# Splitting sets of exponentials between ScalarE and VectorE in a graph-transformer kernel

## The chip, the cores and the metric

The kernel runs on one core of one Trainium2 chip. The metric is device time in microseconds (us): the median of several runs. Engines are named as in the profile: PE is TensorE's matmul, PEld its weight load, ACT is ScalarE, DVE is VectorE, POOL is GpSimd, SP is SyncE, whose queue issues most of the transfers (DMA).

## The reference

Four layers on one graph with N = 3327 nodes, 128 features and a dense float32 matrix `adj`. Each layer ends with a residual and a layer norm. Layer 0 is attention with 128 independent "depths" d and a contraction over 8 heads h; the adjacency is added to the scores twice:

```
h = Wq.shape[0] // d                      # 8
q = (x @ Wq.T).reshape(d, n, h)           # k, v alike
a = jnp.einsum('dnh,dmh->dnm', q, k) * scale
a = a + spatial_encoding + edge_encoding  # both are adj
a = jax.nn.softmax(a, axis=2)
out = jnp.einsum('dnm,dmh->dnh', a, v)
```

So 128 x 3327 x 3327 exponentials are needed, some 1.4 billion. Layers 1 to 3 are products of `adj` (or its transpose) with a 3327 x 128 matrix. Layer 1 scales by the roots of the row sums, layer 2 divides by row sums (`A @ X`) and by column sums (`A.T @ X`), layer 3 has no scaling.

## The kernel before

First a projection stage writes q, k (split into a high and a low part), v and the softmax's row maxima to DRAM. Then comes the attention stage, which this change is about, then a tail: the attention's division and output projection, and four sweeps over `adj`, each in 26 tiles of 128 rows.

**Attention.** A block is a range of CW = 476 queries and one of four ranges of keys (KBS: 7, 7, 6 and 6 tiles of 128 keys); seven query ranges make 28 blocks. Within a block the 128 depths are steps; four steps are a group (GROUP), three groups share one accumulation bank (PACK). In the texts a block with kb = 0 is called full, the other with seven tiles seven, and those with six tiles six. For each step the score tiles, keys on partitions and queries along the row, are made in three sets of PSUM banks `sc[0..2]` (SETS: 3, 2, 2 tiles, or 2, 2, 2). `exponents` does one set: score matmuls (line 632; keys of even and odd tiles stand on different halves of the rows, so two tiles run side by side), then one ACT instruction that takes exp of the whole set (line 640) into the SBUF tile `e`. At a block's first step transposes (line 625) put the adjacency into the banks, and later steps add to what stands there, with the query of the step before taken off again (rows 32 to 63 of `qt`, made by `copy_queries`, lines 517 to 519, in the full blocks and read back from DRAM in the others).

`weigh` does a round: one key tile, four depths, the exponentials times v into the bank `o` (line 658; each of the four column groups is recorded as two matmuls, so a round is x8). A queue holds the previous group's rounds; tables (FULL, PLACES, FIRST) say after which of a group's twelve sets how many rounds are issued. After three groups `flush` adds `o` to `acc` on DVE (lines 669 and 671). `store` writes the sums to `o_s` from POOL's queue.

**DVE's share of the exps.** In three of four groups of a full block, in all of a seven block and in seven of eight of a six block the group's first step gives its whole third set to DVE: `vector_exp` (line 596) reads the two score tiles from PSUM into `ey` as integers scaled for the exponent field, then two bit operations (597, 599) and five polynomial steps (602) follow, each on 128 x 952 elements. The follow-up steps wait in a list and are issued by `vector_work` when two simple clocks allow it.

**Background work.** In the same stage DVE transposes `adj` in 91 pieces of 512 x 256 (lines 218 to 233: transpose, maxima, row sums, column sums), which POOL's queue writes to `adjT_s` (line 253), one piece in eight groups.

**What sets the order.** In attention the order on PE, ACT, DVE and POOL is that of the program text; each instruction waits by semaphore for what it needs, and behind it its engine waits too. `load_heads` brings kt and qt two groups ahead on SP's queue. In the tail only PE and SP are ordered by hand. `gather` (line 1110) is one tile of a sweep: a load of 128 rows of `adjT_s` into one of five buffers, and 26 matmuls. In the first gather sweep DVE and ACT follow each tile with the residual and the norm (lines 1191 to 1077). Column sums are turned into shape before the tail by a small matmul (lines 1035 to 1043).

Of the kernel before, what the change touches and what calls it, by code (L numbers as in the profile page):

```python
# [12 lines left out]
I32 = mybir.dt.int32  # L13
# [17 lines left out]
POLY = (-0.12145248055458069, 1.287218689918518, 0.8447736501693726, 0.7106341123580933, 0.24892811477184296)  # L31
# [19 lines left out]
def kernel(ctx: ExitStack, tc: tile.TileContext, x, adj, wq, wk, wv, wo,  # L51
# [83 lines left out]
    colsum = const.tile([P, T], F32, name="colsum")  # L135
# [20 lines left out]
    csum = const.tile([P, NP // 32], F32, name="csum")  # L156
# [56 lines left out]
    def piece_work(pool, u, c, ai):  # L213

        nj = PIECE // 32
        w = min(PIECE, N - c * PIECE)
        at = pool.tile([P, nj, 4, 32], F32, name="at")
        nc.vector.transpose(at.rearrange("p j t b -> p t j b"), ai.rearrange("p t (j a) -> p t j a", a=32))
        yield at
        if c == 0:  # L220
            maxima[u] = pool.tile([P, 4, NPC], F32, name="pmax")
            sums[u] = pool.tile([P, 4, NPC], F32, name="psum")
        nc.vector.tensor_reduce(maxima[u][:, :, c], ai[:, :, 0:w], AX.X, ALU.max)
        yield at
        nc.vector.tensor_reduce(sums[u][:, :, c], ai[:, :, 0:w], AX.X, ALU.add)
        yield at
        part = csum[:, c * nj:(c + 1) * nj]
        if u == 1:
            nc.vector.tensor_reduce(part, at.rearrange("p j t b -> p j (t b)"), AX.X, ALU.add)
        else:  # L230
            cs = pool.tile([P, nj], F32, name="cs")
            nc.vector.tensor_reduce(cs, at.rearrange("p j t b -> p j (t b)"), AX.X, ALU.add)
            nc.vector.tensor_tensor(part, part, cs, ALU.add)
        yield at

    def store_tops(pool, u, top, n):

        hi = pool.tile([P, 4], F32R, name="rhi")
        nc.vector.tensor_copy(hi, top)
        lo = pool.tile([P, 4], F32R, name="rlo")  # L240
        nc.vector.tensor_tensor(lo, top, hi.bitcast(F32), ALU.subtract)
# [176 lines left out]
    def attention():  # L418
        with tc.tile_pool(name="ed", bufs=1) as ed, tc.tile_pool(name="kq", bufs=3) as kq, \
# [34 lines left out]
            def on_vector(kb, g):  # L454

                return g % 4 != 0 if kb == 0 else KBS[kb][1] == 7 or g % 8 != 0

            FULL = ((0, 2, 4, 4, 7, 7, 9), (0, 0, 3, 7, 7, 10, 10), (0, 0, 3, 6, 6, 9, 9), (0, 0, 3, 6, 7, 10, 10))
            PLACES = {7: (1, 1, 4, 6, 8, 10, 10), 6: (0, 2, 4, 6, 8, 10)}
# [50 lines left out]
            def copy_queries(b, g):  # L513
                qt = heads[b, g][1]
                qf = qt.bitcast(F32)
                before = heads[b, g - 1][1].bitcast(F32)[0:32, GROUP - 1] if g else qf[32:64, 0]
                return [(0.9, None, lambda: nc.vector.tensor_scalar(qt[32:64, 1:], qf[0:32, 0:GROUP - 1], -1.0, None, ALU.mult)),  # L517
                        (0.4, None, lambda: nc.vector.tensor_scalar(qt[32:64, 0], before, -1.0, None, ALU.mult)),
                        (1.2, None, lambda: nc.vector.tensor_copy(qt[64:128], qf[0:64]))]  # L519
# [22 lines left out]
            loaded, worked, turning = [], [], []  # L542

            def background(n):
                if n % PACE == 2 and worked:
                    piece_store(pe, *worked.pop(0))
                if n % PACE == 2 and pieces:
                    u, c = pieces.pop(0)
                    loaded.append((u, c, piece_load(pe, u, c)))

            def background_work(n):
                if n % PACE == 4 and loaded:
                    u, c, ai = loaded.pop(0)
                    steps = piece_work(pe, u, c, ai)
                    worked.append((u, c, next(steps)))
                    next(steps)
                    clock[1] += 2.4
                    turning.append(steps)
                if n % PACE == 0 and turning:
                    clock[1] += 2.4  # L560
                    for _ in turning.pop():
                        pass

            def prepare(b, d):

                n = b * NHG + d // GROUP
                if d % GROUP == 0:
                    while any(of is None for _, of, _ in vec):
                        vec.pop(0)[2]()
# [9 lines left out]
                    background(n)  # L579


                if n + 1 < len(groups) and blocks[groups[n + 1][0]][1] == 0 \
                        and d % GROUP == 1 - on_vector(blocks[b][1], d // GROUP):
                    vec.extend(copy_queries(*groups[n + 1]))
                if d % GROUP == 3:
                    background_work(n)

            vec = []

            def vector_exp(e, x, of):  # L590


                y = ex.tile([P, 2, CW], F32, name="ey")
                t = ex.tile([P, 2, CW], F32, name="et")
                yi, ti = y.bitcast(I32), t.bitcast(I32)
                nc.vector.tensor_scalar(yi, x, -58 * math.log(2.0), 2 ** 24 / math.log(2.0), ALU.max, ALU.mult)  # L596
                vec.append((0.7, of, lambda: nc.vector.tensor_scalar(ti, yi, UPPER, EXPONENT, ALU.bitwise_and,  # L597
                                                                 ALU.bitwise_xor)))
                vec.append((0.7, of, lambda: nc.vector.tensor_scalar(yi, yi, LOWER, QUARTER, ALU.bitwise_and,  # L599
                                                                 ALU.bitwise_or)))  # L600
                for i, a in enumerate(POLY):
                    vec.append((1.2, of, lambda i=i, a=a: nc.vector.scalar_tensor_tensor(  # L602
                        e, e if i else y, a, t if i == len(POLY) - 1 else y, ALU.add, ALU.mult)))

            clock = [0.0, 0.0]

            def vector_work(b):

                while vec and clock[1] < clock[0]:
                    cost, _, step = vec.pop(0)  # L610
                    step()
                    clock[1] += cost
                clock[0] += 0.95 if KBS[blocks[b][1]][1] == 7 else 0.84
                clock[1] = max(clock[1], clock[0] - 1)

            def exponents(b, d, si):
# [3 lines left out]
                s = sc[si]  # L620
                if d == 0:
# [14 lines left out]
                if on_vector(kb, d // GROUP) and (d % GROUP, si) == (0, 2):  # L636
                    vector_exp(e[:, 0:n, :], s[:, 0:n, 0:CW], (b, d // GROUP))
                    clock[1] += 1.2
                else:
                    nc.scalar.activation(e[:, 0:n, :], s[:, 0:n, 0:CW], AF.Exp, scale=2.0)  # L640
# [6 lines left out]
            def weigh(b, g, r):  # L647
# [5 lines left out]

                while any(of == (b, g) for _, of, _ in vec) and r >= SETS[len(queue_of)][2][0]:
                    vec.pop(0)[2]()
                for j in range(GROUP):
# [3 lines left out]
                                     start=(r == 0 and u == 0), stop=(r == nt - 1),  # L660
                                     skip_group_check=True)
                if r == nt - 1 and (u == PACK - 1 or g == NHG - 1):
                    flush(b, g // PACK)

            def flush(b, f):
                kb = blocks[b][1]
                clock[1] += 0.7
# [7 lines left out]
            def store(b, f):  # L675
                nb = min(PACK, NHG - f * PACK)
                for j in range(GROUP):
                    nc.gpsimd.dma_start(  # L678
# [6 lines left out]
            with tc.manual_schedule(engines={mybir.EngineType.PE, mybir.EngineType.Activation,  # L685
# [5 lines left out]
                for _, _, step in copy_queries(*groups[0]):  # L691
                    step()
                values[groups[0]] = load_values(*groups[0])
                for b, d in steps:
# [3 lines left out]
                    for si in range(len(SETS[KBS[blocks[b][1]][1]])):  # L698
                        vector_work(b)
                        exponents(b, d, si)  # L700
                        if queue:
                            at = (FIRST[len(queue_of)] if d < GROUP else PLACES[len(queue_of)] if blocks[b][1] else
                                  FULL[d // GROUP % 4])
                            for _ in range(at.count(place)):
                                weigh(*queue.pop(0))
                        place += 1
                    if d % GROUP == GROUP - 1:
                        while queue:
                            weigh(*queue.pop(0))
                        queue_of = [(b, d // GROUP, r) for r in range(KBS[blocks[b][1]][1])]  # L710
                        queue, place = list(queue_of), 0
                while queue:
                    weigh(*queue.pop(0))
                while stores:
# [320 lines left out]
    pick = act.tile([P, 32], F32, name="pick")  # L1035
    nc.vector.tensor_tensor(pick, ident[:, 0:32], ident[:, 32:64], ALU.add)
    nc.vector.tensor_tensor(pick, pick, ident[:, 64:96], ALU.add)
    nc.vector.tensor_tensor(pick, pick, ident[:, 96:128], ALU.add)
    ps = bank(7)
    nc.tensor.matmul(ps[0:32, 0:NP // 32], lhsT=pick, rhs=csum, start=True, stop=True)  # L1040
    for q in range(4):
        nc.vector.tensor_copy(colsum[32 * q:32 * q + 32, :],
                              ps[0:32, 0:NP // 32].rearrange("a (s q) -> a q s", q=4)[:, q, :])

# [17 lines left out]
    inv_col = inverse_degree(colsum, "inv_col")  # L1062
# [34 lines left out]

    def gather(t, y, col, b, meanwhile=()):
# [13 lines left out]
        for _, what in todo:  # L1112
            what()
        return ps
# [4 lines left out]
    def divide(t):  # L1119
# [7 lines left out]
        nc.gpsimd.tensor_tensor(ons[t][:n], o[:n, 0:H, :], rec[:n, :].unsqueeze(1).to_broadcast([n, H, D]), ALU.mult)  # L1127
# [38 lines left out]
    with tc.manual_schedule(engines={mybir.EngineType.PE, mybir.EngineType.SP}):  # L1166
# [18 lines left out]
        for t in range(T):  # L1185
# [9 lines left out]
            norm(n, h[:n, :], xs[1][:n, t, :])  # L1195

# [77 lines left out]
```

## Time and profile before

| what | us |
|---|---|
| runs, median of 3 | 10735.67 (10734.02 to 10740.07) |
| the profiled execution's own time | 10739.45 |
| its span in the profile | 10737.5 |
| ACT busy in the span | 9584.8 (89%) |
| PE busy | 10565.1 (98%) |
| DVE busy | 7960.2 (74%) |
| POOL busy | 1554.7 (14%) |
| first attention block starts | 316 |
| last flush of attention ends | 9970 |
| first, second, third gather sweep start | 10080, 10396, 10579 |

The granted clock of TensorE was 0.996 of full over the span. How to read the rows: a group of instructions has its line, engine and operation, the tile written and read, shapes and count; then busy time, the mean of one in ns; then the idle time of the engine just before them, and whose work ended it. In rows in order of time there are the start, the length, and the idle time before in brackets. Neighbouring instructions of one line are merged (x8, x16), so the length of a merged row runs from the first start to the last end. The recorded end of a matmul is modelled; its start is not.

### The profile page before, as it was taken

To read this page: it belongs to the slowest core of one execution; us is meant where nothing else is said; L and a number is where in the kernel's file an instruction comes from. 1 tells how busy PE (TensorE), PEld (TensorE's weight loads), DVE (VectorE), ACT (ScalarE), POOL (GpSimd) and SP (SyncE) were. 2 spreads that over 40 slices of the span, in tenths; PEclk is the share of its full clock that TensorE was granted. 3 is DMA by queue.
4 is the path that set the end of the run, shared out by engine and by line. 5 is a ranking of instruction groups with operands and counts; after the bars stand their busy time and mean duration, and the time that the engine had idled before them with its cause. 6 is when DMAs were issued, how large, how long until landed. Compare 5 with 4: busy or idle time off the path is not lost. (4 is left out here: it accounts for less than half of the span.)

```text
span 10737.5 us, 200822 instructions
## 1 busy us (share of the span) xinstructions
PE 10565.1 (98%) x76941; PEld 4105.8 (38%) x76941; DVE 7960.2 (74%) x8554; ACT 9584.8 (89%) x10447; POOL 1554.7 (14%) x2739
## 2 busy tenths in 40 slices
PE   8899999999999999999999999999999999999999
PEld 5333333333333333333333333333333333333779
DVE  6777888777888777887788777888777777777412
ACT  3899999999999999999999999999999999999400
POOL 0111121111221111211122110121111100001200
PEclk9999999999999999999999999999999999999999
DMA  7678886788876888768887588886888867788676
GB/s 270 181 184 188 209 210 181 181 192 201 213 188 171 198 201 209 190 166 200 198 211 196 156 191 191 199 199 172 193 195 202 193 162 179 181 189 196 219 283 246
DMA packets 1013760, 2116.43 MB, mean 197 GB/s; under 512 B 206759, under 2 KB 730985, under 8 KB 998979
## 3 DMA queue, kind: packets, MB, share of 16 engines
q1 hardware_dynamic: 932014, 1985.55, 74.4%
q0 software_dynamic: 79392, 116.16, 3.5%
q8 instruction: 623, 10.21, 0.4%
q14 instruction: 335, 2.74, 0.1%
q10 hardware_dynamic: 1396, 1.77, 0.1%
HBM read 1863.03 MB, written 239.54 MB: 196 GB/s over the span
## 5 line engine op out<-in xcount | busy, mean ns | idle before, releaser
L640 ACT ACTIVATE e<-sc 128x952 f32<-128x952 f32 (+1 forms) x9968 | 9360.0, 1085 | 312.1 <-PE sc L632 284.3
L658 PE MATMUL o<-e,v_pad 128*32 128x476 f32 (+1 forms) x46592 | 5647.1, 573 | 39.4 <-DVE acc L671 18.5
L632 PE MATMUL sc<-qt,kt 64*128 64x476 f32 x23296 | 4491.6, 440 | 52.9 <-ACT e L640 33.5
L632 PEld LDWEIGHTS sc<-qt,kt 64*128 64x128 f32 x23296 | 2184.3, 184 | 4433.6 <-ACT e L640 3740.6
L602 DVE SCALAR_TENSOR_TENSOR e<-e,ey 128x952 f32<-128x952 f32 x2352 | 2707.0, 1151 | 77.4
L596 DVE TENSOR_SCALAR ey<-sc 128x952 int32<-128x952 f32 x784 | 901.1, 1149 | 1411.5 <-PE sc L632 1389.9
L658 PEld LDWEIGHTS o<-e,v_pad 128*32 128x32 f32 (+1 forms) x46592 | 1035.2, 108 | 1907.4 <-issue 1885.1
L533 POOL COPY v_pad<-vs 128x192 f32<-128x192 f32 (+1 forms) x896 | 444.5, 522 | 8018.6 <-DMA vs<-v_img 6214.0
L602 DVE SCALAR_TENSOR_TENSOR e<-ey 128x952 f32<-128x952 f32 x784 | 903.4, 1152 | 27.2
L602 DVE SCALAR_TENSOR_TENSOR e<-e,et 128x952 f32<-128x952 f32 x784 | 901.2, 1149 | 22.3
L253 POOL DMA_DIRECT2D adjT_s<-at x1352 | 760.1, 570 | 132.7 <-DMA adjT_s<-at 92.6
L599 DVE TENSOR_SCALAR ey<-ey 128x952 int32<-128x952 int32 x784 | 519.7, 663 | 27.1
L597 DVE TENSOR_SCALAR et<-ey 128x952 int32<-128x952 int32 x784 | 518.3, 661 | 26.9
L1110 PE MATMUL bank<-y,eT 128*128 128x128 f32 (+1 forms) x4056 | 473.9, 276 | 0.4 <-DVE h L1232 0.4
L1110 PEld LDWEIGHTS bank<-y,eT 128*128 128x128 f32 (+1 forms) x4056 | 465.3, 192 | 5.7 <-DVE h L1232 0.6
L671 DVE TENSOR_TENSOR acc<-o,acc 128x476 f32<-128x476 f32 x231 | 150.3, 651 | 281.5 <-PE o L658 280.9
L517 DVE TENSOR_SCALAR qt<-qt 32x1428 fp32r<-32x1428 f32 x224 | 201.7, 900 | 103.2 <-DMA qt<-q_s 89.2
L519 DVE CAST qt<-qt 64x1904 fp32r<-64x1904 f32 x224 | 260.4, 1163 | 7.6
L1070 ACT ACTIVATE rstd<-mv,eps 128x1 f32<-128x1 f32 x104 | 30.4, 292 | 263.6 <-DVE mv L1068 263.6
L678 POOL DMA_DIRECT2D o_s<-acc x308 | 199.4, 651 | 35.4 <-DVE acc L671 20.8
L1213 PE MATMUL bank<-a,y 128*128 128x512 f32 (+2 forms) x364 | 145.5, 562 | 0.0
L362 ACT ACTIVATE hi<-pp 128x1024 fp32r<-128x1024 f32 x52 | 53.0, 1024 | 87.9 <-PE pp L308 86.3
(148 smaller groups left out, 2274.7 us busy)
## 6 DMA issues: line engine op xcount, KB each, us to landing
qt<-qimg SPq DMA_DIRECT2D x1344, 476.0 KB
kt<-k_s SPq DMA_DIRECT2D x5316, 96.0 KB
kt<-k_s SPq DMA_DIRECT2D x1762, 128.0 KB
eT<-adjT_s SPq DMA_DIRECT2D x78, 1664.0 KB
qimg<-qt SPq DMA_DIRECT2D x224, 476.0 KB
vs<-v_img SPq DMA_DIRECT2D x224, 224.0 KB
adjT_s<-at POOLq DMA_DIRECT2D x1352, 32.0 KB, 4.8
vs<-v_img SPq DMA_DIRECT2D x224, 192.0 KB
```

What stands on the lines that cost most here:

```text
L253: nc.gpsimd.dma_start(out=flat_ap(adjT_s, (t * P + 32 * q) * NP + c * PIECE, [[NP, 32], [P, ns], [1, P]]), in_=at[32 * i:32 * i + 32].rear ...
L517: return [(0.9, None, lambda: nc.vector.tensor_scalar(qt[32:64, 1:], qf[0:32, 0:GROUP - 1], -1.0, None, ALU.mult)), (0.4, None, lambda: nc ...
L519: (1.2, None, lambda: nc.vector.tensor_copy(qt[64:128], qf[0:64]))]
L533: nc.gpsimd.tensor_copy(vp[:, 32:32 + nt * GROUP * 32].rearrange("p (x c) -> p x c", c=32)[:, :, 0:H], vs.rearrange("p (x c) -> p x c", c=H))
L596: nc.vector.tensor_scalar(yi, x, -58 * math.log(2.0), 2 ** 24 / math.log(2.0), ALU.max, ALU.mult)
L597: vec.append((0.7, of, lambda: nc.vector.tensor_scalar(ti, yi, UPPER, EXPONENT, ALU.bitwise_and, ALU.bitwise_xor)))
L599: vec.append((0.7, of, lambda: nc.vector.tensor_scalar(yi, yi, LOWER, QUARTER, ALU.bitwise_and, ALU.bitwise_or)))
L602: vec.append((1.2, of, lambda i=i, a=a: nc.vector.scalar_tensor_tensor(e, e if i else y, a, t if i == len(POLY) - 1 else y, ALU.add, ALU.m ...
L632: nc.tensor.matmul(s[:, i, 0:CW], lhsT=kt[64 * rg:64 * rg + 64, k, pos * P:(pos + 1) * P], rhs=qt[64 * rg:64 * rg + 64, k, :], start=False ...
L640: nc.scalar.activation(e[:, 0:n, :], s[:, 0:n, 0:CW], AF.Exp, scale=2.0)
L658: nc.tensor.matmul(o[32 * j:32 * j + 32, 0:CW], lhsT=values[b, g][:m, c:c + 32], rhs=es[b, g * GROUP + j, r][:m, :], start=(r == 0 and u = ...
L1110: nc.tensor.matmul(ps[:n, 0:D], lhsT=e[:m, s, :n], rhs=y[:m, s, col:col + D], start=(s == 0), stop=(s == T - 1))
```

## The change

- `exponents`: DVE no longer takes whole sets. In a pattern of 36 sets (SHARE; 6 of 36 in full blocks, 8 in seven, 7 in six) ACT does all tiles of a set but the last, and DVE the last, on 128 x 476 elements.
- `vector_exp`: the polynomial has four steps, not five. Its range is shifted by a constant PHASE. `store_tops` puts the shift into the scores, and ACT takes it off again with a constant `bias`.
- The order on DVE: a model in the program keeps times of PE, ACT and DVE (`filled`, `weigh`, `take`, `settle`) and chooses from passes, flushes, copies, and the steps of up to two chains in turn.
- Rounds and the order of key tiles follow tables for three groups (ROUNDS, ORDER).
- A piece of `adj` is three DVE steps, each in a slot of its own; the column sums are no longer made there. Pieces that are left are done in a loop after attention.
- `add_columns` makes the column sums in the first gather sweep from the eT tile that is loaded there; the small matmul and its copies go. `inverse_degree(colsum)` moves behind that sweep.
- The last block's last stores go to the queues of SP and ACT, and the first tile's division is done by DVE instead of POOL.

```diff
-POLY = (-0.12145248055458069, 1.287218689918518, 0.8447736501693726, 0.7106341123580933, 0.24892811477184296)
+POLY = (-0.039287679561190725, 0.7694055213858888, 0.3602062482980112, 0.1471829588776368)
+PHASE = 0.7927868171488225 * math.log(2.0) / 2
...
-        part = csum[:, c * nj:(c + 1) * nj]
...
-        nc.vector.tensor_copy(hi, top)
+        nc.vector.tensor_scalar(hi, top, -PHASE, None, ALU.add)
...
-            def on_vector(kb, g):
-                return g % 4 != 0 if kb == 0 else KBS[kb][1] == 7 or g % 8 != 0
-            FULL = ((0, 2, 4, 4, 7, 7, 9), (0, 0, 3, 7, 7, 10, 10), (0, 0, 3, 6, 6, 9, 9), (0, 0, 3, 6, 7, 10, 10))
-            PLACES = {7: (1, 1, 4, 6, 8, 10, 10), 6: (0, 2, 4, 6, 8, 10)}
+            SHARE = {
+                0: (8, 13, 20, 27, 32, 35),
+                7: (5, 8, 12, 20, 23, 29, 32, 35),
+                6: (4, 8, 13, 19, 25, 31, 35),
+            }
+            ROUNDS = {
+                0: ((1, 1, 0, 0, 2, 0, 0, 2, 0, 0, 1, 0),
+                    (2, 0, 0, 1, 0, 1, 0, 2, 0, 0, 1, 0),
+                    (1, 1, 0, 1, 1, 0, 0, 2, 0, 0, 1, 0)),
+                7: ((0, 2, 0, 0, 2, 0, 0, 1, 0, 1, 1, 0),
+                    (0, 2, 0, 0, 2, 0, 0, 2, 0, 0, 1, 0),
+                    (1, 1, 0, 0, 2, 0, 0, 1, 0, 1, 1, 0)),
+                6: ((0, 1, 0, 2, 0, 0, 1, 0, 1, 0, 1, 0),
+                    (0, 1, 0, 1, 0, 1, 0, 1, 0, 1, 0, 1),
+                    (0, 1, 0, 1, 0, 1, 0, 1, 0, 1, 0, 1)),
+            }
...
+            def on_vector(b, d, si):
+                return (3 * d + si) % 36 in SHARE[kind(b)]
...
+                elif turning and n >= turning[0][2] + 2 and (g % PACK == PACK - 1 or b < len(KBS) and g % (2 * PACK) == 0):
+                    copies.append((now[0], 1.21, "piece", turning[-1].pop(0)))
...
+            def take(limit):
+                at, before = vector
+                first = []
+                if passes and len(chains) < CHAINS:
+                    first.append((max(at, passes[0][0]), "pass"))
+                if flushes:
+                    first.append((max(at, flushes[0][0]), "flush"))
+                start, what = min(first) if first else (limit, None)
+                if what is None or start > at + AHEAD:
+                    if copies and copies[0][0] <= at:
+                        start, what = at, "copy"
+                    elif chains:
+                        chain = chains[1] if len(chains) > 1 and before is chains[0] else chains[0]
+                        start, what = at + (0.117 if before is chain else 0.0), "step"
...
-                if on_vector(kb, d // GROUP) and (d % GROUP, si) == (0, 2):
-                    vector_exp(e[:, 0:n, :], s[:, 0:n, 0:CW], (b, d // GROUP))
-                    clock[1] += 1.2
-                else:
-                    nc.scalar.activation(e[:, 0:n, :], s[:, 0:n, 0:CW], AF.Exp, scale=2.0)
+                own = n - on_vector(b, d, si)
+                nc.scalar.activation(e[:, 0:own, :], s[:, 0:own, 0:CW], AF.Exp, bias=-2 * PHASE, scale=2.0)
...
+                if own < n:
+                    passes.append((at + (0.6, 1.0)[own - 1], (b, d, si),
+                                   lambda e=e, s=s: vector_exp(e[:, own, :], s[:, own, 0:CW])))
...
-                    nc.gpsimd.dma_start(
+                    (nc.gpsimd if not last else (nc.sync, nc.scalar)[j % 2]).dma_start(
...
-        nc.gpsimd.tensor_tensor(ons[t][:n], o[:n, 0:H, :], rec[:n, :].unsqueeze(1).to_broadcast([n, H, D]), ALU.mult)
+        (nc.gpsimd if t else nc.vector).tensor_tensor(ons[t][:n], o[:n, 0:H, :], rec[:n, :].unsqueeze(1).to_broadcast([n, H, D]), ALU.mult)
...
+    def add_columns(t):
+        part = colsum if t == 0 else small.tile([P, T], F32, name="part")
+        nc.vector.tensor_reduce(part, eTs.pop(t), AX.X, ALU.add)
+        if t:
+            nc.vector.tensor_tensor(colsum, colsum, part, ALU.add)
...
             norm(n, h[:n, :], xs[1][:n, t, :])
+            add_columns(t)
+        inv_col = inverse_degree(colsum, "inv_col")
```

## The prediction

> **What bounds the kernel now.** I read the page first. PE is busy 98% of the span and ACT 89%, but a matmul's recorded end is modelled, so that 98% is no proof. The costliest groups are those of the attention stage:
>
> ```profile
> L640 ACT ACTIVATE e<-sc 128x952 f32<-128x952 f32 (+1 forms) x9968 | 9360.0, 1085 | 312.1 <-PE sc L632 284.3
> ...
> L602 DVE SCALAR_TENSOR_TENSOR e<-e,ey 128x952 f32<-128x952 f32 x2352 | 2707.0, 1151 | 77.4
> L596 DVE TENSOR_SCALAR ey<-sc 128x952 int32<-128x952 f32 x784 | 901.1, 1149 | 1411.5 <-PE sc L632 1389.9
> ...
> L671 DVE TENSOR_TENSOR acc<-o,acc 128x476 f32<-128x476 f32 x231 | 150.3, 651 | 281.5 <-PE o L658 280.9
> ```
>
> 10,752 sets of exps (28 blocks x 128 steps x 3 sets), 9968 on ACT and 784 on DVE. Next the stretches of the four blocks of one query range, in the order full (kb 0, seven tiles), seven (kb 1), six, six. Columns: length, then busy time of PE, PEld, DVE, ACT, POOL, the clock, the DMA share.
>
> ```profile
> 7216.50:7584.30 367.80, 360.74 (x2709) 129.12 (x2708) 298.43 (x318) 363.65 (x361) 57.74 (x104) 1.00 0.67 175
> 7584.30:7951.90 367.60, 366.69 (x2714) 130.38 (x2712) 288.12 (x288) 355.99 (x352) 51.04 (x98) 1.00 0.82 191
> 7951.90:8272.70 320.80, 319.06 (x2340) 105.23 (x2338) 254.65 (x270) 308.47 (x357) 51.65 (x96) 1.00 0.85 203
> 8272.70:8591.40 318.70, 318.46 (x2333) 105.58 (x2332) 237.88 (x238) 308.85 (x357) 35.84 (x68) 1.00 0.83 195
> ```
>
> The four make 1374.9 us; attention is seven such ranges (from 316 to 9970). Next the order of time, of ACT in a seven block and in a six block:
>
> ```profile
> 5007.55 11.12 ACT L640 ACTIVATE e<-sc 128x1428 f32<-128x1428 f32 x11 [0.39 <-PE sc L632]
> 5018.91 11.12 ACT L640 ACTIVATE e<-sc 128x1428 f32<-128x1428 f32 x11 [0.24 <-PE sc L632]
> ...
> 8026.56 19.81 ACT L640 ACTIVATE e<-sc 128x952 f32<-128x952 f32 x23 [0.30 <-PE sc L632]
> 8046.68 9.53 ACT L640 ACTIVATE e<-sc 128x952 f32<-128x952 f32 x11 [0.30 <-PE sc L632]
> ```
>
> Where ACT doesn't wait, exps start 0.844 us apart after two tiles and 1.241 after three (medians of the starts), so a tile is worth 0.397 and an instruction 0.05. A group of four steps in a seven block repeats every 11.36 us (5007.55 to 5018.91). Its eleven exps are worth 4 x 1.241 + 7 x 0.844 = 10.87: ACT lacks work for 0.49. The 23 exps from 8026.56 take 20.12 to the next start. That is a group with no vector set (12 exps, 10.13 of work, 10.29 from start to start) and one with (11 exps, 9.28 of work, 9.83). So a whole set moved to DVE takes 0.844 from ACT and shortens the group by 0.46. The gap comes at the set that skips ACT. PE, same group:
>
> ```profile
> 5003.42 1.30 PE L632 MATMUL sc<-qt,kt 64*128 64x476 f32 x7
> 5004.80 1.80 PE L658 MATMUL o<-e,v_pad 128*32 128x476 f32 x16
> 5006.54 1.16 PE L632 MATMUL sc<-qt,kt 64*128 64x476 f32 x7
> 5007.62 1.01 PE L658 MATMUL o<-e,v_pad 128*32 128x476 f32 x8
> 5008.56 1.10 PE L632 MATMUL sc<-qt,kt 64*128 64x476 f32 x5
> 5009.59 1.01 PE L658 MATMUL o<-e,v_pad 128*32 128x476 f32 x8
> 5010.53 0.70 PE L632 MATMUL sc<-qt,kt 64*128 64x476 f32 x4
> 5011.15 1.01 PE L658 MATMUL o<-e,v_pad 128*32 128x476 f32 x8
> ```
>
> A round (x8) is followed by scores 0.94 after its start, in all 4757 cases, so PE never waits there. It waits inside fills: seven tiles take 1.38 before the round at 5004.80 and 1.08 at 5006.54. A second round starts 0.82 after the first; the scores of one row half follow each other at 0.216 (0.32 the first time after a round); the round comes 0.30 after the last fill. A burst of rounds thus costs 0.30 + 0.94 - 0.82 + 0.10 - 0.216 = 0.305 beyond its rounds. PE's own work of a seven group is 7 x 0.823 + 16 x 0.216 + 5 bursts x 0.305 = 10.75, of a six group 6 x 0.823 + 12 x 0.219 + 6 x 0.305 = 9.40. **PE and ACT are nearly equal, and each waits for the other**: 5% of the time is neither's work.
>
> **The change, part by part.**
>
> *ACT.* Of each 36 sets, 6 (full), 8 (seven) or 7 (six) give one tile to DVE; no set skips ACT any more. Tiles per block: 63, 85, 74. ACT's work of a block, all sets, is 128 x (1.241 + 2 x 0.844) = 374.9 or 128 x 3 x 0.844 = 324.1. Before, less 0.844 for 24, 32 and 28 sets: 354.7, 347.9, 300.5. After, less 0.397 a tile: 349.9, 341.2, 294.7. That is 5 to 7 us a block.
>
> The added `bias` stands against this. The Trainium skill (ScalarE: Activation LUTs, What ACT_TABLE_LOAD costs) prices a bias read through a pointer at 93 ns more; L1070, which reads `eps` so, takes 292 ns for one element. By that rule 10,752 exps would pay 1000 us. But the bias here is a Python number, like the `scale=2.0` beside it, and I take nothing for it.
>
> *PE.* The same matmuls. Counting bursts in the tables: full 4.5 a group before, 5.33 after; seven 5 and 5; six 6 and 5.67. So PE's work becomes 5.76 + 3.46 + 1.63 = 10.85 (full), 10.75 (seven), 9.29 (six); per block 347, 344, 297. It gains nothing; only its waits can go.
>
> *DVE.* Rows at 952 and 476 columns (1151 and 651 ns) give a fixed 151 ns and 500 per 476 columns, so the integer steps of 661 ns become about 406. What counts is the distance of starts:
>
> ```profile
> 5010.89 2.33 DVE L602 SCALAR_TENSOR_TENSOR e<-e,ey 128x952 f32<-128x952 f32 x2
> 5013.14 1.21 DVE L225 TENSOR_REDUCE psum<-ai 128x4 f32<-128x1024 f32 x1
> 5014.27 1.21 DVE L232 TENSOR_REDUCE cs<-at 128x8 f32<-128x1024 f32 x1
> ```
>
> Two dependent steps: 1.18 for a 1.15 step (+0.03). Two independent ones: 1.13 for 1.21 (-0.08). The skill (VectorE: DVE Perf Modes, The DRAIN you can't avoid) says that the next operation doesn't start until the pipe is empty. By it a tile costs 0.685 + 2 x 0.44 + 4 x 0.685 = 4.31, and alternating two chains is useless. By the row, alternated chains cost 0.57 + 2 x 0.33 + 4 x 0.57 = 3.51; the old chain, one tile of two, 4.24. I take 3.51 with 4.31 as the other end. Per block, with flushes (11 x 0.57), piece steps (10 x 1.16) and in full blocks the query copies (32 x 2.42): full 316, seven 316, six 278, if alternated; 367, 384, 337 if not. Against PE's and ACT's 350, 344, 297 DVE is 90 to 94% loaded; before it was 75 to 81% busy.
>
> *Column sums.* They leave attention (1.2 us a piece, no limit there), and return as a 3.62 us reduce (L411 takes 3616 ns for 3327 elements) and a 0.2 us add per tile of the first gather. There VectorE idles 4.2 us of each 6.35 (before L1191, waiting for PE), so they are hidden with 0.3 us to spare; without this cover, 26 x 3.8 = 99 us. The eT buffer is held 6 us longer of the 32 that five make. Nothing.
>
> *Pieces.* 91 x 3 steps have 64 + 240 = 304 slots, so the loop at the end should be empty. *Tail.* The first division by VectorE and the last stores on two queues spare one POOL operation: 2.4 us to nothing, I take 2. DMA stays as it is, two groups ahead; its share of 0.85 rises by 3%.
>
> **The sum.** Time of a block = the largest engine's work x (1 + loss) + 2.6 us at its ends. The loss now is (367.8 - 2.6) / 354.7: 3.0% (full), 4.9% (seven), 5.9% (six). No skipping set remains, which is where the gaps lie, and the group without one loses only 1.6% (10.29 for 10.13). Against that, PE is now as loaded as ACT, DVE nearly, and a half set is free only when two engines have read it. Ends: 1% and the old loss. I take 2.5%, near the group that skips nothing. Full 349.9 x 1.025 + 2.6 = 361.3, seven 344 x 1.025 + 2.6 = 355.2, six 297 x 1.025 + 2.6 = 307.0: 6.5, 12.4, 13.8 and 11.7 us less, 44.4 a range, 311 in seven. The profiled execution took 10,739.45 (span 10,737.5), 3.8 above the median of the runs. 10,739 - 311 - 2 = 10,426.
>
> **Rivals.** (A) The above, 10,426; between 2 and 3% of loss, 10,385 to 10,475: 57%. (B) The loss stays: three engines tie each other as two did. 363.0, 363.5, 317.1, 317.1: 14 a range, 10,637. For it: PE has not a microsecond less to do, and bursts grow in the full blocks. Against: the group at 8026.56. 20%. (C) Loss 1%: 10,290. 10%. (D) **Slower: VectorE's fixed order.** Its instructions stand in the order of a model; where a pass from PSUM stands ahead of its scores, all behind it waits, and PE then waits for the bank. DVE's sum is 1188 a range, so 187 us are free below the present 1375: 0.63 us for each of 296 tiles. Beyond that it is slower, by 207 us for each further 0.1. Chains that never alternate lose 0.8. Today L596 waits 1411.5 / 784 = 1.8 us each, but with slack to wait in. At 0.7: 10,880. 9%. (E) The change doesn't do what it says: the bias is read through a pointer: about 11,400. 1%. Within 0.2%: 3%.
>
> **Numbers.** 0.2% is about what a measurement here can tell from none. Faster A + B + C = 0.87, same 0.03, slower 0.10. The range leaves out (E), most of (D) and the outer half of (C): 10,290 to 10,690.
>
> **What would show it.** Right: L640's successor 10,752 times with a 476-column form, and a one-tile set 0.45 us behind its predecessor; 2072 passes on DVE; blocks near 361, 355, 307; starts of ACT with gaps under 0.3 us a group; the fills' waits for ACT gone. Wrong: DVE over 97% busy in a block, PE waiting for the vector pass (D); gaps of 0.5 a group as before (B); ACT steps of 0.94 (E); a z in the first gather that starts later than 6.35 us after the last; pieces after attention.

## The result and the profile after

The changed kernel takes 11,137.11 us (median of four runs, 11,130.17 to 11,155.81); the kernel before, run beside it, 10,737.87. The ratio is 1.0375, with an interval of 1.0357 to 1.0393: 3.75% slower, where the prediction had 2.9% faster. Its profiled execution took 11,139.46, with a span of 11,137.4; the mean granted clock of TensorE fell from 0.996 to 0.970.

The span grew by 399.9 us. Attention, from the first score matmul to the last, went from 9647.7 to 9973.6 us (+326). The first gather sweep, measured from its start to the start of the next, went from 315.6 to 382.0 us (+66). Some 8 us are left, nearly all of it behind the start of the last matmul (6.4 us before, 14.1 after): the closing DRAIN on POOL's queue lasts 2.7 us before and 10.5 after. Why it grew stays open.

The costliest groups of the changed kernel (busy time, mean duration in ns, then the idle time of the engine just before these instructions and what ended most of it):

```profile
L728 ACT ACTIVATE e<-sc 128x952 f32<-128x952 f32 (+2 forms) x10752 | 9237.3, 992 | 761.4 <-PE sc L723 688.3
...
L723 PE MATMUL sc<-qt,kt 64*128 64x476 f32 x23296 | 4354.1, 440 | 465.4 <-DVE ey L617 446.1
...
L617 DVE TENSOR_SCALAR ey<-sc 128x476 int32<-128x476 f32 x2072 | 1348.7, 651 | 631.8 <-ACT e L728 600.2
...
L217 DVE STREAM_TRANSPOSE at<-ai 128x1024 f32<-128x1024 f32 x91 | 113.3, 1245 | 454.7 <-DMA kt<-k_s 202.1
```

The counts are as forecast: 10,752 exps on ACT and 2072 passes on VectorE. ACT's busy time fell by 123 us (it was 9360.0), but its wait for scores grew from 312 to 761. PE itself now stands idle 446 us ahead of scores until VectorE has read a bank (`ey`, L617). And the transposes of 91 adjacency pieces, 1.2 us each, have 454.7 us of idle VectorE ahead of them; before, the same group (then at L218) had 0.7. The two sums nearly agree, as those of one stall seen from two engines would; the first experiment below bears this out.

The stretches of the four blocks of one query range (length, then busy time of PE, PEld, DVE, ACT and POOL, the granted clock, the DMA share and GB/s):

```profile
7509.20:7885.60 376.40, 367.25 (x2709) 133.57 (x2708) 329.99 (x556) 359.05 (x384) 45.30 (x65) 0.99 0.62 162
7885.60:8246.30 360.70, 358.76 (x2716) 132.44 (x2714) 323.31 (x613) 352.59 (x385) 39.17 (x73) 1.00 0.88 192
8246.30:8579.40 333.10, 313.42 (x2337) 99.45 (x2336) 290.40 (x547) 303.60 (x385) 48.54 (x97) 0.97 0.86 196
8579.40:8922.60 343.20, 315.17 (x2334) 99.90 (x2332) 291.79 (x544) 304.05 (x384) 66.20 (x119) 0.96 0.83 192
```

The seven block in the second row, with a clock of 1.00, is 6.9 us shorter than before. The two six blocks are 12 and 24 us longer, though ACT is busy 5 us less in each of them and VectorE only 87 and 85% of the time. So no engine became the bound by its load. The last two blocks of the kernel have no pieces left to turn:

```profile
9673.00:9983.00 310.00, 309.06 (x2336) 98.20 (x2335) 289.84 (x537) 303.18 (x385) 14.62 (x33) 1.00 0.89 198
9983.00:10290.00 307.00, 305.46 (x2308) 97.08 (x2310) 284.21 (x524) 300.42 (x382) 40.29 (x72) 1.00 0.85 190
```

The same two blocks before the change, which had no pieces either:

```profile
9327.70:9647.20 319.50, 319.26 (x2339) 105.28 (x2338) 236.31 (x235) 308.26 (x357) 10.70 (x31) 1.00 0.83 192
9647.00:9964.00 317.00, 316.76 (x2321) 104.19 (x2319) 235.22 (x235) 307.15 (x355) 38.88 (x72) 1.00 0.79 184
```

With the same exps, the same tables and no pieces, a six block takes 310 and 307 us, against 319.5 and 317 before and a forecast of 307.0. Here the half sets do what was worked out; something about the pieces seems to take it back.

**One stall.** Four stretches around a typical one, columns as above:

```profile
1200.00:1214.00 14.00, 13.98 (x108) 4.32 (x100) 11.69 (x23) 14.00 (x19) 5.09 (x10) 1.00 1.03 236
1214.00:1227.30 13.30, 1.61 (x12) 0.45 (x12) 2.73 (x5) 2.31 (x4) 4.86 (x10) 0.63 0.78 188
1227.30:1231.00 3.70, 3.62 (x16) 1.20 (x16) 3.63 (x9) 1.82 (x2) 0.00 (x0) 0.50 0.00 0
1231.00:1240.00 9.00, 9.00 (x72) 2.73 (x70) 7.35 (x14) 8.29 (x11) 0.35 (x1) 0.99 0.49 110
```

For 13.3 us all compute engines do next to nothing. The same moment in order of time (start, duration, instruction; in brackets the idle time before it and what ended it), VectorE and PE:

```profile
1211.49 0.64 DVE L627 SCALAR_TENSOR_TENSOR e<-e,et 128x476 f32<-128x476 f32 x1
1214.60 1.00 PE L763 MATMUL o<-e,v_pad 128*32 128x476 f32 x8
1224.54 1.25 DVE L217 STREAM_TRANSPOSE at<-ai 128x1024 f32<-128x1024 f32 x1 [12.40 <-DMA adjT_s<-at]
1227.38 1.16 PE L723 MATMUL sc<-qt,kt 64*128 64x476 f32 x4 [11.77 <-DVE ey L617]
1228.47 1.81 PE L763 MATMUL o<-e,v_pad 128*32 128x476 f32 x8
```

and POOL, whose queue issues the stores of a piece:

```profile
1205.76 0.87 POOL L551 COPY v_pad<-vs 128x192 f32<-128x192 f32 x1 [14.69 <-DMA vs<-v_img]
1206.58 3.69 POOL L244 DMA_DIRECT2D adjT_s<-at  x7
1212.30 0.54 POOL L244 DMA_DIRECT2D adjT_s<-at  x1 [2.03 <-issue]
1213.95 4.21 POOL L244 DMA_DIRECT2D adjT_s<-at  x8 [1.11 <-DMA adjT_s<-at]
```

The cause is read from POOL's rows, and the runs below test it. POOL waits 14.69 us for a transfer of values before it can copy them (L551). Only then does it issue the 16 stores of the last piece, out of the one buffer `at`; the last is issued by 1218.2. The next transpose, which writes into the same `at`, has been at the head of VectorE's queue since 1212.1 and starts at 1224.54, 6.4 us after that last issue. Behind it stand the passes that would free banks; PE fills what is free and stops at 1215.6, then ACT runs dry. In the whole trace 57 of the 91 transposes wait over 0.7 us. 51 of these, with 429 of the 455 us, start 0.1 to 0.6 us after the last of the 16 stores has landed. In the 57, POOL's copy ahead of the stores had waited 17.8 us (median); in the other 33 that follow a store, 0.0. POOL's copies wait for values in both kernels (6214 us in all before, 6582 after); new is that stores of a piece stand behind such a wait. Groups that otherwise mostly last 9.3 to 11.6 us mostly last 20 to 24 with a wait of over 7 us.

**The gather sweep**, VectorE in order of time:

```profile
10441.46 0.35 DVE L1188 TENSOR_SCALAR x<-h,mv,rstd 128x128 f32<-128x128 f32 x1
...
10445.25 3.62 DVE L1211 TENSOR_REDUCE part<-eT 128x26 f32<-128x3328 f32 x1 [3.44 <-DMA eT<-adjT_s]
10448.78 0.28 DVE L1311 TENSOR_TENSOR z<-bank,y 128x128 f32<-128x128 f32 x1
```

The reduce at 10445.25 belongs to tile 7, whose eT is still being loaded; the addition at 10448.78 belongs to tile 3. The reduce was put ahead of that addition. VectorE waits 3.44 us for the transfer and then works 3.62; tile 3's last matmul starts at 10445.48, so its sums stand ready for some 3 us. At tile 5 they were ready before the reduce in front had begun (last matmul at 10462.34, reduce at 10463.06). PE in turn waits for the norms (2.53 us at 10450.96). From tile 5 to tile 23 its tiles start 6.35 and 11.4 to 13.6 us apart in turn, instead of 6.35 throughout.

### The profile page after: what moved, and what is told of

Read it like the earlier page. It is cut to its first block, busy times and chain, and to the rows that moved or that the text cites. A ratio compares the mean times of both kernels' runs of the same rounds, so it can differ in the third digit from the quotient of the medians.

```text
span 11137.4 us, 209915 instructions
## 1 busy us (share of the span) xinstructions
PE 10540.7 (95%) x76939; PEld 4100.4 (37%) x76939; DVE 9123.3 (82%) x16662; ACT 9459.9 (85%) x11231; POOL 1554.4 (14%) x2734
## 5 line engine op out<-in xcount | busy, mean ns | idle before, releaser
L728 ACT ACTIVATE e<-sc 128x952 f32<-128x952 f32 (+2 forms) x10752 | 9237.3, 992 | 761.4 <-PE sc L723 688.3
L763 PE MATMUL o<-e,v_pad 128*32 128x476 f32 (+1 forms) x46592 | 5728.5, 579 | 5.1 <-POOL v_pad L551 3.0
L723 PE MATMUL sc<-qt,kt 64*128 64x476 f32 x23296 | 4354.1, 440 | 465.4 <-DVE ey L617 446.1
L627 DVE SCALAR_TENSOR_TENSOR e<-e,ey 128x476 f32<-128x476 f32 x4144 | 2667.0, 650 | 36.4
L617 DVE TENSOR_SCALAR ey<-sc 128x476 int32<-128x476 f32 x2072 | 1348.7, 651 | 631.8 <-ACT e L728 600.2
L551 POOL COPY v_pad<-vs 128x192 f32<-128x192 f32 (+1 forms) x896 | 477.9, 553 | 8303.4 <-DMA vs<-v_img 6581.8
L627 DVE SCALAR_TENSOR_TENSOR e<-ey 128x476 f32<-128x476 f32 x2072 | 1344.8, 652 | 28.5
L627 DVE SCALAR_TENSOR_TENSOR e<-e,et 128x476 f32<-128x476 f32 x2072 | 1344.6, 651 | 7.8
L624 DVE TENSOR_SCALAR ey<-ey 128x476 int32<-128x476 int32 x2072 | 843.9, 410 | 14.0
L621 DVE TENSOR_SCALAR et<-ey 128x476 int32<-128x476 int32 x2072 | 843.6, 410 | 11.0
L217 DVE STREAM_TRANSPOSE at<-ai 128x1024 f32<-128x1024 f32 x91 | 113.3, 1245 | 454.7 <-DMA kt<-k_s 202.1
```

Of the source, the lines that this page charges most:

```text
L551: nc.gpsimd.tensor_copy(vp[:, 32:32 + nt * GROUP * 32].rearrange("p (x c) -> p x c", c=32)[:, :, 0:H], vs.rearrange("p (x c) -> p x c", c=H))
L621: nc.vector.tensor_scalar(parts["t"].bitcast(I32), yi, UPPER, EXPONENT, ALU.bitwise_and, ALU.bitwise_xor)
L627: nc.vector.scalar_tensor_tensor(e, e if i else y, POLY[i], parts["t"] if i == len(POLY) - 1 else y, ALU.add, ALU.mult)
L723: nc.tensor.matmul(s[:, i, 0:CW], lhsT=kt[64 * rg:64 * rg + 64, k, pos * P:(pos + 1) * P], rhs=qt[64 * rg:64 * rg + 64, k, :], start=False ...
L728: nc.scalar.activation(e[:, 0:own, :], s[:, 0:own, 0:CW], AF.Exp, bias=-2 * PHASE, scale=2.0)
L763: nc.tensor.matmul(o[32 * j:32 * j + 32, 0:CW], lhsT=values[b, g][:m, c:c + 32], rhs=es[b, g * GROUP + j, r][:m, :], start=first and u == ...
```

## The experiments

Two theories were set against others. For attention: the stores of `at` are late (S), or the load of `ai` (L), or VectorE has too much work in too fixed an order (O). For the sweep: a reduce put ahead holds the additions (H), or the eT buffers are held too long (B).

**A second buffer for the transposed piece.**

```diff
-        at = pool.tile([P, nj, 4, 32], F32, name="at")
+        at = pool.tile([P, nj, 4, 32], F32, name="at", bufs=2)
```

> The changed kernel with a second buffer for at, the transposed piece; nothing else. Theory S (the piece's transpose stands at the head of VectorE's queue until POOL has stored the piece before it, out of the one buffer at): the idle time of VectorE before the transpose (455 us) falls below 100, PE's idle before scores (465 us) likewise, and the kernel takes 11,137 - 350 to 420, about 10,750. Rival L (it stands there for the load of its own piece, ai): no change, about 11,130. Rival O (VectorE, 82% busy over the span, is simply overloaded, and the stalls are passes in the wrong place): under 50 us less, and the waits move from the transpose to the passes.

Measured: 10,679.82 us, ratio to before 0.9951 (0.9935 to 0.9968). One argument is worth 457 us and turns the change into a gain. The groups of the scores and of the transposes:

```profile
L723 PE MATMUL sc<-qt,kt 64*128 64x476 f32 x23296 | 4313.4, 436 | 96.3 <-DVE ey L617 76.3
...
L217 DVE STREAM_TRANSPOSE at<-ai 128x1024 f32<-128x1024 f32 x91 | 113.0, 1241 | 46.0 <-POOL ai L196 22.9 <-DMA ai<-in_adj_dram 19.0 <-DMA kt<-k_s 1.6
```

The idle time ahead of the transposes falls from 454.7 to 46.0, and PE's ahead of scores from 465.4 to 96.3. None of the ten waits over 0.7 us that are left ends with the landing of the stores; most of what is left comes from the load and from the memset by POOL (L196) that stands ahead of it for pieces at the edge. Attention takes 9508.4 us. The tables, the half sets and VectorE's order are unchanged, so O can't be the cause of these 457 us.

**The load one piece ahead**, with a single `at`:

```diff
-        ai = pool.tile([P, 4, PIECE], F32, name="ai")
+        ai = pool.tile([P, 4, PIECE], F32, name="ai", bufs=2)
...
-                    work = piece_work(pe, u, c, piece_load(pe, u, c))
+                    work = piece_work(pe, u, c, ahead.pop() if ahead else piece_load(pe, u, c))
+                    if pieces:
+                        ahead.append(piece_load(pe, *pieces[0]))
```

> The changed kernel with two buffers for ai, and each piece loaded one whole piece ahead; one buffer at, as in the change. Theory S: little change, 11,050 to 11,140; only the thirteen pieces of the last rows, whose loads wait for a memset by POOL, gain. Rival L: idle before the transpose gone, about 10,750. Rival O: no change.

Measured: 11,110.67 us, ratio 1.0353 (1.0336 to 1.0371).

```profile
L217 DVE STREAM_TRANSPOSE at<-ai 128x1024 f32<-128x1024 f32 x91 | 113.2, 1244 | 409.7 <-DMA kt<-k_s 260.8 <-DMA adjT_s<-at 89.5 <-DMA vs<-v_img 43.6
```

The load accounts for 45 us of idle time and 26 us of run time, and the stall stays. L falls. Of the releasers named here only `adjT_s` is the store; `kt` and `vs` are other transfers that end near the same time. A label is not enough; the two runs are what tells the store from the load.

**The stores issued ahead of the values.** If the stores are late because they stand behind POOL's copy of values, it is enough to issue them first, with one buffer:

```diff
-                if turning and not turning[-1]:
-                    piece_store(pe, *turning[0][:2], turned[0])
-                    turning.clear()
...
+                    if turning and not turning[-1] and not any(key == "piece" for _, _, key, _ in copies):
+                        piece_store(pe, *turning[0][:2], turned[0])
+                        turning.clear()
                     if n + 1 < len(groups):
                         values[groups[n + 1]] = load_values(*groups[n + 1])
```

Theory S2 is this one; S3 says that the stores themselves take too long, wherever they are issued.

> The changed kernel, one buffer at, but the piece's sixteen stores are put ahead of load_values on POOL's queue instead of behind it. Theory S2 (POOL issues the stores late because they stand behind a copy into v_pad that waits for a vs transfer of the same group, which is so in every second group): the stores start some 10 us earlier where they were late, idle before the transpose falls from 455 us to under 150, kernel 10,750 to 10,850. Rival S3 (sixteen stores at 0.56 us and their landing take too long wherever they start): less than 100 us gained.

Measured: 10,680.48 us, ratio 0.9945 (0.9929 to 0.9962): as much as the second buffer, and better than expected. S2 stands, S3 falls.

```profile
L217 DVE STREAM_TRANSPOSE at<-ai 128x1024 f32<-128x1024 f32 x91 | 113.0, 1242 | 48.6 <-DMA kt<-k_s 23.3 <-DMA ai<-in_adj_dram 14.7 <-DMA adjT_s<-at 8.5
```

**The kernel before, with its piece steps moved earlier in the group.** If the distance from store to reuse were the whole cause, the old kernel should stall too once its piece step comes at the group's first step instead of its last:

```diff
-                if d % GROUP == 3:
+                if d % GROUP == 0:
                     background_work(n)
```

> The kernel before, with one number changed: the piece's work is put at the first step of its group and not at the fourth, so that it comes two groups after the load and the stores and not two and three quarters. No half sets, no new tables, VectorE 74% busy. Theories S and L: the transpose now waits here too, though less than in the changed kernel, because the old order issues the step later behind the list of polynomial steps: 100 to 400 us of idle before it, and a kernel of 10,800 to 11,100. Rival O: same as before within 20 us, since VectorE has slack.

Measured: 10,767.6 us, ratio 1.0029 (1.0018 to 1.0040).

```profile
L218 DVE STREAM_TRANSPOSE at<-ai 128x1024 f32<-128x1024 f32 x91 | 112.8, 1240 | 52.0 <-DMA kt<-k_s 35.2 <-DMA adjT_s<-at 10.4 <-DMA lead_s<-rhi 6.3
```

A miss: 52 us of idle time at 16 transposes, where 100 to 400 were expected. 15 of the 16 start within 0.5 us of the landing of the last store, so it is the same wait, but a rare and short one. VectorE now reaches the transpose 9.0 us after the start of the last store's issue (15.6 in the kernel before, 2.4 in the changed one, medians). From that issue to the start of the transpose it is 6.4 us in the changed kernel's 57 long waits (median), which fit into 9.0. In the old kernel pieces begin only in groups of one parity, and in those the values are already there, so POOL's copy doesn't hold the stores. The stall of 455 us needs both, two groups between store and reuse, and late stores: this run has the two groups without late stores, the run with two buffers has late stores and a longer distance. The old kernel had neither, and its earlier steps cost it some 30 us in all.

**The order in the sweep.** The loop of the first gather sweep is put under a manual schedule for VectorE, so that its instructions stand as the program has them:

```diff
+        with tc.manual_schedule(engines={mybir.EngineType.DVE}):
+            for t in range(T):
-        for t in range(T):
...
```

> The changed kernel with VectorE in program order in the first gather sweep, so that the reduce for column sums comes behind the norm of its own tile and not three or four tiles ahead of it, where it waits for a transfer. Theory H (the reduce of a tile still in transfer holds up the additions behind it): from the sweep's start to the start of the third layer's sweep 316 us as before instead of 382, total 11,137 - 66 = 11,071. Rival B (the reduce keeps the eT buffers longer, so that loads come late): no more than 15 us less. Attention is untouched by either.

Measured: 11,058.23 us, ratio 1.0300 (1.0283 to 1.0317), 79 us less than the changed kernel. VectorE in this sweep, in order of time:

```profile
10436.69 3.61 DVE L1211 TENSOR_REDUCE part<-eT 128x26 f32<-128x3328 f32 x1
10440.33 0.19 DVE L1213 TENSOR_TENSOR colsum<-colsum,part 128x26 f32<-128x26 f32 x1
10440.99 0.29 DVE L1312 TENSOR_TENSOR z<-bank,y 128x128 f32<-128x128 f32 x1 [0.47 <-PE bank L1229]
```

The reduce no longer waits for a transfer, and the addition after it waits 0.47 us for PE, which is the slack that the prediction put at 0.3. A `z` comes every 6.35 us again, and the sweep takes 315.6 us as before: 66 of the 79 us. H stands. B falls: here the reduce stands behind the norm of its own tile, so the buffers are held at least as long.

**Both mends together**, the second `at` and the sweep's order.

> The changed kernel with both cures: two buffers for at, and VectorE in program order in the first gather sweep. Theories S and H: the two losses lie in different stages and add up, 10,680 - 79 = 10,600, 1.2% below the kernel before. If they were one loss seen twice: about 10,660.

Measured: 10,612.41 us, ratio 0.9882 (0.9866 to 0.9899). The single effects, 457 and 79, would make 10,601; the two causes are nearly independent. On this kernel the next two runs take away what the change is about.

**No half sets**: all exps on ScalarE.

```diff
-                0: (8, 13, 20, 27, 32, 35),
-                7: (5, 8, 12, 20, 23, 29, 32, 35),
-                6: (4, 8, 13, 19, 25, 31, 35),
+                0: (),
+                7: (),
+                6: (),
```

> The kernel with both cures, but no set shares a tile with VectorE: ScalarE does all exps, the tables of rounds stay. By the engines' sums ScalarE has 374.9, 374.9 and 324.1 us of work in a block against 349.9, 341.2, 294.7, and PE, with 344 to 347 and 297, has room: loss 1 to 2%, blocks of 381, 381, 331; a query range 1424, and the kernel 10,600 + 7 x (1424 - 1343) = 11,170. If the half sets were worth nothing: 10,600.

Measured: 11,120.92 us, ratio 1.0355 (1.0338 to 1.0372). The half sets are worth 508 us against none at all, with the tables of rounds left as they are for half sets; tables fitted to this kernel were not run. The shares of the engines:

```profile
PE 10860.8 (98%) x76939; PEld 4148.7 (37%) x76939; DVE 1534.5 (14%) x2158; ACT 10178.3 (92%) x11231; POOL 1387.2 (12%) x2734
```

Blocks take 382.2, 381.8 and 333.8 us (medians, from one block's start to the next), 1.9, 1.8 and 3.0% above ACT's own work of 374.9, 374.9 and 324.1. PE's recorded 98% says little here: the blocks follow ACT's work, while PE's, as the prediction summed it, is 344 to 347 and 297.

**One chain on VectorE instead of two.**

```diff
-            AHEAD, CHAINS = 0.5, 2
+            AHEAD, CHAINS = 0.5, 1
```

> The kernel with both cures, but one chain of polynomial steps at a time instead of two in turn (CHAINS = 1). By the distances of starts (0.57 for an independent step, 0.685 for one that waits for the step before it) a tile costs VectorE 4.3 us and not 3.5, its sum in a block rises to 367, 384, 337, it becomes the bound: 1425 to 1480 a query range, kernel 11,170 to 11,560. If alternating were useless (a step never starts before the one before it has drained): no change, 10,600.

Measured: 12,219.91 us, ratio 1.1379 (1.1360 to 1.1398), well above the expected range. The chain is not only slower by its dependent steps. PE's waits show the rest (instruction, what it waited for, us in total, times, longest):

```profile
PEld sc L723 <- DVE ey L617: 2795.3, 1940, 5.2
...
PE sc L723 <- DVE ey L617: 1258.7, 952, 4.4
```

`CHAINS` is also the number of buffers of `ey` and `et`, which falls to one. With one chain the next pass out of PSUM may start only when the last chain is done, and PE's loads wait 1940 times for one of the 2072 passes. The run can't separate the two parts, so it gives no price for dependent steps alone. A query range takes some 1586 us here, 243 more than four undisturbed blocks (1343.1, below). As an estimate, the 1425 to 1480 expected for dependent steps alone explain 82 to 137 of that, and 106 to 161 are left for held passes. So rival D was near: an order of VectorE's that holds the passes can cost a large part of the 1608 us between the two runs.

**All three mends**: the stores first, two `at` buffers and the sweep's order.

> The changed kernel with VectorE in program order in the first gather sweep, two buffers for at, and the stores ahead of load_values on POOL's queue. Either of the last two takes away the wait for the stores, so they don't add up: what is left before the transpose (46 us with two buffers alone) falls by some 20, 10,580 to 10,610.

Measured: 10,576.76 us, ratio to before 0.9849 (0.9836 to 0.9863), slightly better than expected and the fastest version here: 162 us less than the kernel before beside it and 560 less than the changed one. The transposes, and the same four blocks as above (columns as there):

```profile
L217 DVE STREAM_TRANSPOSE at<-ai 128x1024 f32<-128x1024 f32 x91 | 113.0, 1242 | 16.9 <-DMA ai<-in_adj_dram 12.6 <-DMA kt<-k_s 2.2 <-issue 1.0
```

```profile
7086.20:7454.80 368.60, 364.59 (x2711) 132.67 (x2710) 330.17 (x557) 358.81 (x384) 48.41 (x65) 1.00 0.63 164
7454.80:7814.50 359.70, 358.96 (x2713) 132.40 (x2712) 323.55 (x613) 352.37 (x385) 41.35 (x74) 1.00 0.88 194
7814.50:8124.40 309.90, 309.50 (x2340) 98.73 (x2338) 290.70 (x547) 303.03 (x385) 51.08 (x97) 1.00 0.92 211
8124.40:8437.50 313.10, 309.18 (x2335) 98.79 (x2334) 291.08 (x543) 303.07 (x384) 69.54 (x119) 1.00 0.90 211
```

Busy times of VectorE and ACT are those of the changed kernel to within 1 us; the blocks are 7.8, 1.0, 23.2 and 30.1 us shorter, and the clock is 1.00 in each.

## Why the prediction was wrong

**The step that failed** is the line on the pieces: "91 x 3 steps have 64 + 240 = 304 slots, so the loop at the end should be empty", with its companion, "DMA stays as it is". The loop was indeed empty (the last transpose is at 9366.9, inside attention). But a slot was counted as if it cost its 1.16 us and nothing else. Two things about it were never costed: how soon after its stores the buffer `at` is written again, and what stands ahead of those stores on POOL. The change moved both, and the transpose then held VectorE's queue at its head, 57 times. Measured in its place: 455 us of idle time ahead of the transposes; 457 us of run time by either cure.

**Rival D had the right kind of failure and the wrong instruction.** It said that VectorE's order is fixed, that what waits at the head holds all behind it, and that PE then waits for the bank. All of that is in the trace. But it put the waiting at the passes, priced it by their number, and tied it to a VectorE busy for over 97%. VectorE was 85 to 90% busy. The instruction that waits is one of 91, not one of 2072, and it waits for a transfer.

**Column sums: "hidden with 0.3 us to spare".** The size was right: 0.47 us in the run with the program's order. What failed was the silent premise that VectorE runs this sweep in the order of the text. It is not ordered by hand there, and reduces that wait for a load were put ahead of additions. The cover was gone for a part of the tiles, and 66 us came of the 99 that the prediction named for no cover at all. The sign that it gave for this, a `z` later than 6.35 us after the last, is what the trace has.

**ACT: right.** The next step starts 1.240, 0.844 and 0.463 us after one of three, two and one tile (medians; 0.446 is the commonest for one tile); the prediction had 1.241, 0.844 and 0.45. So the immediate `bias` costs nothing here, and rival E is out. This agrees with the Trainium skill (ScalarE: Activation LUTs, What ACT_TABLE_LOAD costs), which puts its 93 ns on a pointer operand and not on an immediate one.

**VectorE: right within 5%.** Steps of two alternating chains start 0.564 us apart (0.57 was taken), against 0.688 where a polynomial step follows its own predecessor, about a fifth of those that have one. The next independent operation starts before a 0.65 us one is over. The prediction set its row against the rule of the Trainium skill (VectorE: DVE Perf Modes, The DRAIN you can't avoid) and left out the end of that paragraph, which says that a next operation that isn't held starts earlier. So page and row don't differ, and the page does not make alternating useless. Busy time is 330, 323 and 290 us in the stretches, where 316, 316 and 278 were summed.

**The loss: a term of the wrong size.** Blocks that no stall touches (in the run with the second `at` alone) take 362.9, 359.6 and 310.3 us (the third block of a range stands for both six blocks; the end of the fourth comes below), against 361.3, 355.2 and 307.0. Less 2.6 us at the ends, that is 3.0, 3.8 and 3.6% above the largest engine's work, not 2.5%: between cases A and B. Four such blocks make 1343.1 us, 12.6 more than forecast, and 88 us in seven ranges.

**The account.** Seven ranges took 9647.7 us before, 1378.2 each. Undisturbed blocks would save 7 x 35.1 = 246 us of that (223 of seven ranges like the one that the prediction used, 1374.9: its 311 less the 88). Attention instead grew by 326: the disturbances cost 572, of which either cure of the stores wins back 457. The best version saves 183, so some 63 us of disturbance are left in it. Ahead of the transposes 17 us of them are seen in its trace. And the last group of a range's fourth block takes 12.4 to 14.7 us there, in each of the first six ranges, against 10.2 to 10.7 before, some 20 us in all; in the changed kernel's trace the query copies of the next range stand ahead of a pass at this place. That was read, not tested. What the rest is stays open.

## What to carry to other kernels

When a background step is put in the queue of an in-order engine, cost its waits as well as its duration: for each buffer that it writes, the time from the issue of the last transfer out of it to the next write, and what stands ahead of that transfer on the queue that issues it. Work of 1.2 us that waits 12 can cost some 12 on every engine behind it, though VectorE, in whose queue it stands, is busy less than 90% of the time. A label of a wait for several semaphores names only the last; a second buffer on one side and an earlier load on the other tell which it was.

## What the runs showed of the hardware

A stall costs more than its length, because TensorE comes back slower. In the stretches of the stall above the granted clock is 0.50 for the 3.7 us after PE's 11.77 us of idle time, and a round of eight matmuls takes 1.81 us instead of 1.00. In the attention stage of the changed kernel the first round after an idle time of 0.1 to 2 us takes 1.0 us in 97 of 107 cases; after more than 3.4 us it takes 1.81 (38 of 39 cases, the other 1.62), and between the two there are both. The kernel before has only two idle times over 2 us in attention, of 2.9 us in the mean, so its profile gave hardly a hint of it. The granted clock is 0.50 in 56 stretches of attention, 549.5 us in all (before: 4 stretches, 44.4 us), and each lasts a multiple of 3.41 us. The Trainium skill (TensorE: Matmul & The Clock Gate, Part 1: The HAM clock gate) says the same: half rate after an idle window of about 3.4 us, and full rate again after about as long a busy one. In these stretches PE is recorded as busy for 283 us (before: 24.5). As an estimate, half of the difference, 129 us, is what the slow clock costs, a part of the 572.
